# Row maxima transposed in float32 and split when they leave PSUM, and gelu rows evicted by ScalarE, in a gated attention and mixing kernel

## The chip, the cores and the metric

The kernel runs on one core of a Trainium2 chip. The metric is the device time of one launch in microseconds, as the median of several runs. A core has TensorE (PE, its weight loads shown as PEld), VectorE (DVE), ScalarE (ACT), GpSimd (POOL), and SyncE (SP), which here only issues DMAs. Each engine works through its own queue in order and waits on semaphores for the others.

## The reference, cut to what matters

`x` is 8 x 512 x 2048, `ctx` has the same shape. Two layers follow each other, each with a layernorm over the 2048 columns in front and a gated addition behind:

```python
x = x + tanh(g_xattn[0]) * xattn(layernorm(x), ctx, mask, Wq, bq, Wk, bk, Wv, bv, Wo, bo)
x = x + tanh(g_ffn[0]) * ffn(layernorm(x), W_res, W_pre, W_post, ..., W_branch)
```

The attention cuts the 2048 columns into patches of 128. In a patch, q and k come from the normalised x and v from ctx; 8 heads of 32 channels attend within the patch:

```python
scores = einsum('bhdi,bhdj->bhij', qh, kh) / sqrt(dh)
scores = where(mask > 0, scores, -1e9)
attn = softmax(scores, axis=-1)
o = gelu(einsum('bhij,bhdj->bhdi', attn, vh).reshape(BN, DK, W), approximate=False)
out = einsum('de,bew->bdw', Wo, o) + bo[:, None]
```

The second layer takes each row of 2048 as 4 streams of 512. It computes 24 logits of a row (16 for a 4x4 matrix, 4 + 4 for two softmaxes), makes the matrix doubly stochastic by 50 Sinkhorn iterations, and mixes the streams with it. A weighted sum of the streams goes through `W_branch` and is added to each stream with its own weight.

## The kernel before, in words

The work is cut into 32 blocks of 512 columns (`n`), 4 per batch element, and each block into 4 patches of 128 columns, 128 patches in all (`t`). One loop runs over `t` and, for each, goes through the string `ORDER = "MeoaMgPlsMMvSMpOM"`, whose letters call the stages: `s` the score maxima of patch `t + 3` (`smax`), `e` the exponentials of patch `t` (`expo`), `a` the sums over values of patch `t - 1` (`attv`), `g`, `o` and `O` the output projection of the block before (`outp`), `p` and `P` the q and k projection of a later block (`proj`) and its restacking through DRAM (`stack`), `v` the value projection (`vproj`), `S` the row sums and logits of a later batch element (`stats`), `M` steps of the mixing of an earlier batch element (`mix`). At the last block of a batch element its logits are finished (`rawmap`) and its Sinkhorn chain (`ffn`) is put in at a priority of its own. A scheduler then orders each engine's instructions by priority and by its own model of times, so the order of every queue is made anew whenever an instruction changes.

**Score maxima.** `smax` multiplies the stacked q and k of a patch (16-bit, 97 rows) head by head into one PSUM tile `sc` of 128 x 8 x 128 (L569, 8 matmuls) and VectorE takes the maximum over each row (L571, `mx`, 128 rows x 8 heads). VectorE scales it and rounds it to float16 (L573), and takes the rest that this loses as a second float16 part (L574); both lie in `mq`, 128 x 16. TensorE transposes `mq` into the first 16 partitions of the same `sc` tile, seen as float16 (L576), and ScalarE copies that to `mh`, 16 x 128 (L578). Two DMAs on SyncE's queue put the two halves of `mh` into rows 97 and 98 of the stacked q (L582). `expo` then multiplies 99 rows (L595, tile `sT`), so that the row maximum is subtracted within the matmul, and ScalarE takes the exponential (L597, `e`). `sc` and `sT` come from one pool of two PSUM buffers (`ps_s`).

**Projection.** For each quarter of the q and k rows TensorE makes 12 matmuls (L518 to L520) into `qk`, ScalarE writes the first float16 part of the result (L522) and VectorE the second (L523, both into `ev`). The activations are split the same way before: GpSimd normalises (L500, `xn`), ScalarE casts (L505, `xh`), GpSimd subtracts (L507, `xl`).

**Attention.** TensorE sums the exponentials and their products with the values (L612, L616, tile `u`), ScalarE makes the reciprocal by a logarithm and an exponential (L618, L619, `rc`), and VectorE multiplies (L620, `o`).

**Output.** ScalarE applies gelu to a block of `o` (L627) between two loads of its function table, GpSimd multiplies by the mask (L632). TensorE transposes the 8 squares of 128 x 128 in two groups (L641, `gTp`, in the pool `ps_t` of two PSUM buffers), and VectorE copies each group of 128 x 512 to `gT` (L642). Four matmuls with the logit weights follow (L645). ScalarE rounds `o` (L655, `gh`), GpSimd takes the rest (L657, `gl`), TensorE makes the output projection (L667 to L670), VectorE adds it to x (L671), ScalarE sums the squares (L673).

**Second layer.** A Sinkhorn sweep is six small VectorE instructions (L844, L846, L848, L850, L852, L854) that depend on each other; 49 sweeps for each of 8 batch elements. The mixing uses VectorE (L946, L949), ScalarE (L939) and GpSimd (L944); for some tiles of the late batch elements it runs on TensorE instead (L1000, L1001).

Of the kernel before, what the change touches and what calls it, by code (L numbers as in the profile page):

```python
# [11 lines left out]
F16 = mybir.dt.float16  # L12
BF16 = mybir.dt.bfloat16
AF = mybir.ActivationFunctionType
ALU = mybir.AluOpType
# [4 lines left out]
P = 128  # L20
D = 512
S = 2048
DK = 256
NH = 8
# [12 lines left out]
MH_ACT = False  # L37
# [54 lines left out]
M_UNIT = 16384.0  # L92
# [7 lines left out]
def gated_xattn_mhc_kernel(  # L100
# [21 lines left out]
    V, A, G, T, SY = nc.vector, nc.scalar, nc.gpsimd, nc.tensor, nc.sync  # L122
# [6 lines left out]
    def ctile(shape, dt, name):  # L129
        return const.tile(shape, dt, tag=name, name=name)  # L130


    ident = ctile([P, P], F32, "ident")
# [8 lines left out]
    ident16 = ctile([P, P], F16, "ident16")  # L142
# [49 lines left out]
    mp = ctx.enter_context(tc.tile_pool(name="mp", bufs=BUF_MP))  # L192
# [10 lines left out]
    def defer(k, tag, fn):  # L203
        if k == 0:
            fn()
        else:
            late.append([k, fn, tag])
# [49 lines left out]
    with tc.tile_pool(name="set", bufs=1) as st:  # L257

        def stile(shape, dt, name, tag=None):
            return st.tile(shape, dt, tag=tag or name, name=name)  # L260
# [64 lines left out]
        for t in range(2):  # L325
            sl = slice(256 * t, 256 * t + 256)
# [21 lines left out]
        mh = stile([B * 16, 3, P], BF16, "mh")  # L348
# [213 lines left out]
    def smax(t):  # L562

        m, p = divmod(t, PSB)
        q, kk = QS[m % NS], KS[m % NS]
        sl = slice(p * P, (p + 1) * P)
        sc = ps_s.tile([P, NH, P], F32, tag="s", name="smax")
        for h in range(NH):
            T.matmul(sc[:, h, :], q[0:97, h, sl], kk[0:97, h, sl], start=True, stop=True)  # L569
        mx = mp.tile([P, NH], F32, tag="mx", name="mx")  # L570
        V.tensor_reduce(mx, sc, AX.X, ALU.max)  # L571
        mq = mp.tile([P, 2, NH], F16, tag="mq", name="mq")
        V.tensor_scalar(mq[:, 0, :], mx, 1.0 / M_UNIT, None, ALU.mult)  # L573
        V.scalar_tensor_tensor(mq[:, 1, :], mx, 1.0 / M_UNIT, mq[:, 0, :], ALU.mult, ALU.subtract)  # L574
        mt = sc[0 : 2 * NH, 0, :].bitcast(F16)[:, 0:P]
        T.transpose(mt, mq.rearrange("p r h -> p (r h)"), ident16)  # L576
        mh = mp.tile([2 * NH, P], F16, tag="mh", name="mh")
        A.copy(mh, mt)  # L578

        def put():  # L580
            for r in range(2):
                (A if MH_ACT else SY).dma_start(q[97 + r : 98 + r, :, sl], mh[r * NH : (r + 1) * NH, :])  # L582

        defer(D_MH, t, put)

# [36 lines left out]
    def outp(n):  # L622

        b, k = divmod(n, NBLK)
        o = ob.pop(n)
        for g in range(2):
            gi = A.activation(o[:, g], o[:, g], AF.Gelu, bias=bvc[:, g : g + 1])  # L627
        with tc.issue_after(gi.ins), tc.high_priority():
            A.preload_act_table_set(EXP_SET)
        mb = gp.tile([P, BLK], F32, tag="mb", name="mb")  # L630
        SY.dma_start(mb, mask[b, k * BLK : (k + 1) * BLK].partition_broadcast(P))
        G.tensor_tensor(o, o, mb.unsqueeze(1).broadcast_to([P, 2, BLK]), ALU.mult)  # L632
        j0 = n * NP
        gt_ = op_.tile([P, NP, DK + 1], F32, tag="gT", name="gT")
        G.tensor_copy(gt_[:, :, DK], maskT[:, j0 : j0 + NP])
        yield
        for q in range(2):
            pt = ps_t.tile([P, 2, 2, P], F32, tag="t", name="gTp")
            for j in range(2):
                for e in range(2):  # L640
                    T.transpose(pt[:, j, e, :], o[:, e, (2 * q + j) * P : (2 * q + j + 1) * P], ident)  # L641
            V.tensor_copy(gt_[:, 2 * q : 2 * q + 2, 0:DK], pt.rearrange("p j e s -> p j (e s)"))  # L642
        g4 = ps_t.tile([P, DK + 1], F32, tag="t", name="g4")
        for p in range(NP):
            T.matmul(g4[32 * p : 32 * p + 32, :], Wm[:, k * NP + p, :], gt_[:, p, :], start=True, stop=True)  # L645
        if k == 0:
            g4s = lnp.tile([P, DK + 1], F32, tag="g4s", name="g4s", bufs=2)
            V.tensor_copy(g4s, g4)
            G4[b] = g4s
        else:  # L650
            V.tensor_tensor(G4[b], g4, G4[b], ALU.add)
        mr = MR[n % 2]
        SY.dma_start(mr[0:6, :], mrow_d[:, n * BLK : (n + 1) * BLK])
        gh = gp.tile([P, 2, BLK], F32R, tag="gh", name="gh")
        A.copy(gh, o)  # L655
        gl = gp.tile([P, 2, BLK], F32R, tag="gl", name="gl")
        G.tensor_tensor(gl, o, gh.bitcast(F32), ALU.subtract)  # L657
        if k == 0:
            sq2[b] = lnp.tile([P, 4, NBLK], F32, tag="sq2", name="sq2")
            x1s[b] = x1d.tile([D, S], F32, tag="x1s", name="x1s")  # L660
        xt = xtile.pop(n)
        yield
        for c in range(4):
            ps = ps_p.tile([P, BLK], F32, tag="p", name="op")
            cs = slice(c * P, (c + 1) * P)
            for e in range(2):
                T.matmul(ps, WoH[:, e, cs], gh[:, e], start=(e == 0), stop=False)  # L667
                T.matmul(ps, WoH[:, e, cs], gl[:, e], start=False, stop=False)  # L668
                T.matmul(ps, WoL[:, e, cs], gh[:, e], start=False, stop=False)  # L669
            T.matmul(ps, bo6[:, cs], mr, start=False, stop=True)  # L670
            V.tensor_tensor(xt[c], ps, xt[c], ALU.add)  # L671
            jk = fp.tile([P, BLK], BF16, tag="ph", name="junk2", bufs=BUF_PH)
            A.activation(jk, xt[c], AF.Square, bias=nmean[b][:, c : c + 1], accum_out=sq2[b][:, c, k : k + 1])  # L673
            defer(D_X1, "x1", lambda cs=cs, c=c: SY.dma_start(x1s[b][cs, k * BLK : (k + 1) * BLK], xt[c]))
            yield
# [341 lines left out]
    for t in range(2):  # L1017
        smax(t)
# [4 lines left out]
    for t in range(2, AHEAD):  # L1023
        smax(t)
# [22 lines left out]
    def act(c, t):  # L1047
# [8 lines left out]
        elif c == "a" and 1 <= t <= NT_:  # L1056
            at("attv", attv, t - 1)
        elif c == "g" and p == 0 and n >= 1:
            og_[0] = outp(n - 1)
            at("outp", next, og_[0])  # L1060
        elif c == "P" and live_ and n + 1 < NTOT:
# [6 lines left out]
        elif c == "l" and live_:  # L1068
# [4 lines left out]
            if p == LXP and n > 1 and n + 2 < NTOT:  # L1073
                defer(D_LX, "lx", lambda n=n: load_x(n + 2))
        elif c == "s" and live_ and t + AHEAD < NT_:
            at("smax", smax, t + AHEAD)
        elif c == "v" and live_:
            if t + 2 < NT_ and t % 2 == 0:
# [117 lines left out]
```

## Time and profile before

| what | us |
|---|---|
| median of 3 runs | 1831.41 |
| lowest and highest of them | 1829.26, 1835.13 |
| the profiled execution | 1828.05 |
| its span, first to last instruction | 1825.9 |
| mean granted TensorE clock | 0.932 of full speed |
| score maxima (L571), first and last start | 73.0, 1595.7 |

The profile is of one execution on the core. A row of instructions names the line, the engine, the operation, the tile written and the tiles read, the shapes, how many there are, their busy time and mean duration, and then how long the engine sat idle before them and who ended that. A row of waits names the one that waits, the one that ended the wait, the total in us, how many times, and the longest. A slice row gives the busy share of an engine in 40 equal slices of the span, in tenths, where 9 is 90% or more; one slice is 45.6 us. The ends of TensorE's matmuls are modelled, so their rows can overlap. The score maxima end near 1600 us; what follows is the last Sinkhorn chain and the mixing of the last batch elements.

### The profile page before, as it was taken

What the parts mean: (1) busy time and instruction counts of PE and PEld (TensorE: products, weight loads), DVE (VectorE), ACT (ScalarE), POOL (GpSimd) and SP (SyncE); (2) the same over time, 40 slices, a digit from 0 to 9 for tenths busy, and PEclk for the clock granted to TensorE, in tenths of its full rate; (3) what the DMA queues carried; (4) which work ended last, traced back from release to release, by engine and by line L of the source; (5) the groups of instructions that cost most, each with busy time, mean ns of one, the idle gap of its engine ahead of it and who ended that gap; (6) DMA issues with size and microseconds to landing.
All of it is one profiled execution on the core that took longest, in us unless ns stands there. A gap on an engine that the chain in (4) does not pass through costs nothing.

```text
span 1825.9 us, 32268 instructions
## 1 busy us (share of the span) xinstructions
PE 1547.1 (85%) x10517; PEld 901.0 (49%) x10517; DVE 1382.3 (76%) x4201; ACT 1069.4 (59%) x2030; POOL 602.8 (33%) x511
## 2 busy tenths in 40 slices
PE   3998999989889888889878888799888889768887
PEld 2554555555555554545544445455455555543333
DVE  7434345877888778888888879889898998998761
ACT  2386466646555656558565475566665566755454
POOL 0512222322232243342444333444334442321121
PEclk7999999999999988999988999899999999989999
DMA  6478696467646855568555784468755565523443
GB/s 214 139 209 256 208 258 194 140 174 232 180 134 200 254 169 165 151 192 269 162 154 164 214 251 144 139 196 259 215 154 165 148 189 147 172 93 119 144 157 117
DMA packets 353237, 330.60 MB, mean 181 GB/s; under 512 B 53351, under 2 KB 251303, under 8 KB 353070
## 3 DMA queue, kind: packets, MB, share of 16 engines
q1 hardware_dynamic: 353070, 328.55, 60.6%
q8 instruction: 83, 1.36, 0.3%
q14 instruction: 84, 0.69, 0.1%
HBM read 226.71 MB, written 101.16 MB: 180 GB/s over the span
## 4 chain that ended last, share of the span: by engine, by line
PE 37%; DVE 23%; DMA 18%; issue 9%; ACT 9%; POOL 4%; SPq 1%; ACTq 0%; POOLq 0%; DVEq 0%
PE vp L559 5%; DVE w L946 4%; DMA xs<-in_x_dram 4%; PE qk L518 3%; PE qk L519 3%; DMA out_dram<-w 3%; PE qk L520 3%; DMA x<-x1s 2%; PE mx L1000 2%; DMA x1s<-xt 2%; PE lgx L448 2%; DVE mx L571 2%; PE op L667 2%; DVE W L844 2%; PE mx L1001 2%
## 5 line engine op out<-in xcount | busy, mean ns | idle before, releaser
L559 PE MATMUL vp<-Wv,ct 128*128 128x256 f32 x1024 | 272.4, 418 | 16.7 <-DMA ct<-in_cx_dram 15.1
L500 POOL TENSOR_SCALAR xn<-xt,ln_r,nb 128x512 f32<-128x512 f32 x128 | 105.5, 826 | 501.2 <-DMA xt<-in_x_dram 385.7
L559 PEld LDWEIGHTS vp<-Wv,ct 128*128 128x128 f32 x1024 | 207.4, 210 | 68.0 <-issue 18.6
L518 PE MATMUL qk<-xh,WqkH 128*128 128x512 f16 x512 | 199.2, 390 | 29.4 <-ACT xh L505 16.3
L946 DVE SCALAR_TENSOR_TENSOR w<-x,Et,w 128x512 f32<-128x512 f32 x180 | 180.0, 1001 | 49.6 <-POOL w L944 34.0
L519 PE MATMUL qk<-xl,WqkH 128*128 128x512 f16 x512 | 197.9, 387 | 4.3 <-POOL xl L507 4.0
L520 PE MATMUL qk<-xh,WqkL 128*128 128x512 f16 x512 | 197.6, 386 | 0.0
L571 DVE TENSOR_REDUCE mx<-smax 128x8 f32<-128x1024 f32 x128 | 154.9, 1210 | 41.7 <-PE smax L569 41.3
L507 POOL TENSOR_TENSOR xl<-xn,xh 128x512 f16<-128x512 f32 x128 | 156.3, 1228 | 76.0 <-ACT xh L505 70.4
L597 ACT ACTIVATE e<-sT,ebi,esc 128x1024 f32<-128x1024 f32 x128 | 153.4, 1198 | 18.0 <-PE sT L595 17.9
L523 DVE SCALAR_TENSOR_TENSOR ev<-qk,bqs,ev 128x512 f16<-128x512 f32 x128 | 94.5, 739 | 77.5 <-ACT ev L522 76.1
L667 PE MATMUL op<-gh,WoH 128*128 128x512 f32 x256 | 120.9, 474 | 35.3 <-DVE ev L523 31.1
L944 POOL TENSOR_TENSOR w<-w,pj 128x512 f32<-128x512 f32 x60 | 80.1, 1334 | 213.1 <-ACT w L939 113.7
L505 ACT CAST xh<-xn 128x512 f16<-128x512 f32 x128 | 78.3, 612 | 103.7 <-POOL xn L500 102.9
L522 ACT ACTIVATE ev<-qk,bqs 128x512 f16<-128x512 f32 x128 | 86.9, 679 | 85.0 <-PE qk L520 78.7
L673 ACT ACTIVATE junk<-xt,nmean 128x512 bf16<-128x512 f32 x128 | 91.6, 716 | 73.9 <-DVE xt L671 41.3
L850 DVE TENSOR_TENSOR W<-E,uv 128x64 f32<-128x64 f32 x392 | 119.4, 307 | 5.4
L844 DVE TENSOR_TENSOR W<-E,uv 128x64 f32<-128x64 f32 x352 | 117.1, 335 | 4.8
L612 PE MATMUL u<-e,onesb 128*32 128x256 f32 x1024 | 102.7, 403 | 10.5 <-DVE mq L573 3.8
L668 PE MATMUL op<-gl,WoH 128*128 128x512 f32 x256 | 107.1, 418 | 0.0
L669 PE MATMUL op<-gh,WoL 128*128 128x512 f32 x256 | 106.6, 417 | 0.0
L632 POOL TENSOR_TENSOR o<-o,mb 128x1024 f32<-128x1024 f32 x32 | 75.6, 2364 | 93.2 <-ACT o L627 85.9
(287 smaller groups left out, 3504.6 us busy)
## 6 DMA issues: line engine op xcount, KB each, us to landing
xt<-in_x_dram SPq DMA_DIRECT2D x128, 256.0 KB
ct<-in_cx_dram SPq DMA_DIRECT2D x128, 256.0 KB
xTt<-in_xT_dram SPq DMA_DIRECT2D x128, 256.0 KB
qd<-ev SPq DMA_DIRECT2D x128, 256.0 KB
x1s<-xt SPq DMA_DIRECT2D x128, 256.0 KB
xs<-in_x_dram SPq DMA_DIRECT2D x112, 256.0 KB
QS<-qd SPq DMA_DIRECT2D x192, 128.0 KB
KS<-qd SPq DMA_DIRECT2D x192, 128.0 KB
```

The source lines that it names most:

```text
L507: G.tensor_tensor(l, xn, h, ALU.subtract)
L518: T.matmul(ps, WqkH[:, c, ms], hs[c], start=(c == 0), stop=False)
L519: T.matmul(ps, WqkH[:, c, ms], ls[c], start=False, stop=False)
L520: T.matmul(ps, WqkL[:, c, ms], hs[c], start=False, stop=(c == 3))
L559: T.matmul(ps[:, h, :], ct[:, c, :], Wv[:, c, :], start=(c == 0), stop=(c == 3))
L571: V.tensor_reduce(mx, sc, AX.X, ALU.max)
L597: A.activation(e32, sc, AF.Exp, bias=ebi[:, t : t + 1], scale=esc[:, t : t + 1])
L667: T.matmul(ps, WoH[:, e, cs], gh[:, e], start=(e == 0), stop=False)
L668: T.matmul(ps, WoH[:, e, cs], gl[:, e], start=False, stop=False)
L844: V.tensor_tensor(W4[:, h], E4[:, h], vb[:, h], ALU.mult)
L850: V.tensor_tensor(W4[:, h], E4[:, h], ub[:, h], ALU.mult)
L946: V.scalar_tensor_tensor(w, x1[j], E[:, n, 4 * j + i : 4 * j + i + 1], w, ALU.mult, ALU.add)
```

## The change

Two places change.

In `smax`, the maxima go to TensorE as they are, in float32, and come out of PSUM in two float16 parts. ScalarE scales and rounds while it copies; VectorE then computes the rest from the same PSUM rows and ScalarE's part. The tile `mq` and its two VectorE instructions are gone. `mh` is now 8 partitions x 2 x 128, and each DMA takes one part of it.

In `outp`, the transposed gelu rows are copied out of PSUM by ScalarE and not by VectorE.

```diff
         mx = mp.tile([P, NH], F32, tag="mx", name="mx")
         V.tensor_reduce(mx, sc, AX.X, ALU.max)
-        mq = mp.tile([P, 2, NH], F16, tag="mq", name="mq")
-        V.tensor_scalar(mq[:, 0, :], mx, 1.0 / M_UNIT, None, ALU.mult)
-        V.scalar_tensor_tensor(mq[:, 1, :], mx, 1.0 / M_UNIT, mq[:, 0, :], ALU.mult, ALU.subtract)
-        mt = sc[0 : 2 * NH, 0, :].bitcast(F16)[:, 0:P]
-        T.transpose(mt, mq.rearrange("p r h -> p (r h)"), ident16)
-        mh = mp.tile([2 * NH, P], F16, tag="mh", name="mh")
-        A.copy(mh, mt)
+
+        mt = sc[0:NH, 0, :]
+        T.transpose(mt, mx, ident)
+        mh = mp.tile([NH, 2, P], F16, tag="mh", name="mh")
+        A.activation(mh[:, 0, :], mt, AF.Copy, scale=1.0 / M_UNIT)
+        V.scalar_tensor_tensor(mh[:, 1, :], mt, 1.0 / M_UNIT, mh[:, 0, :], ALU.mult, ALU.subtract)
 
         def put():
             for r in range(2):
-                (A if MH_ACT else SY).dma_start(q[97 + r : 98 + r, :, sl], mh[r * NH : (r + 1) * NH, :])
+                (A if MH_ACT else SY).dma_start(q[97 + r : 98 + r, :, sl], mh[:, r, :])
...
-            V.tensor_copy(gt_[:, 2 * q : 2 * q + 2, 0:DK], pt.rearrange("p j e s -> p j (e s)"))
+            A.copy(gt_[:, 2 * q : 2 * q + 2, 0:DK], pt.rearrange("p j e s -> p j (e s)"))
```

In the changed kernel the transpose is L574, ScalarE's part L576, VectorE's L577 and the DMAs L581; lines further down stand one lower than before, so the gelu copy is L641.

## The prediction

> **What bounds the kernel now.** I read the page's busy shares first, then the slices, then one steady stretch by itself, and last who ends TensorE's idle time in it. The busy shares and two of the slice rows:
>
> ```profile
> PE 1547.1 (85%) x10517; PEld 901.0 (49%) x10517; DVE 1382.3 (76%) x4201; ACT 1069.4 (59%) x2030; POOL 602.8 (33%) x511
> PE   3998999989889888889878888799888889768887
> DVE  7434345877888778888888879889898998998761
> ```
>
> TensorE looks like the bound, but its ends are modelled. Start to start, two 16-bit matmuls of 512 columns lie 0.216 us apart where their rows show 0.39 us, so its 85% is overstated. VectorE's rows hardly overlap, and from the eighth slice on it is at 7 tenths or more, mostly 8 or 9, until the last two. The stretch from 330 to 1530 us, where attention tiles, projections, the Sinkhorn sweeps and the mixing of a finished batch all interleave, by itself:
>
> ```profile
> 330.00:1530.00 1200.00, 1026.69 (x7353) 624.63 (x7352) 1010.28 (x2939) 730.48 (x1407) 452.65 (x371) 0.93 0.63 186
> ```
>
> The columns are length, busy PE, PEld, DVE, ACT, POOL, granted clock, DMA share, GB/s. VectorE works 1010 of 1200 us; 190 us are left. TensorE's waits in the stretch that bear on this change (total us, times, longest):
>
> ```profile
> PE op L667 <- DVE ev L523: 29.5, 20, 4.9
> PE g L645 <- DVE gT L642: 17.2, 10, 3.9
> PE smax L576 <- DVE mq L574: 6.3, 4, 3.3
> ```
>
> Adding all of TensorE's waits of the stretch by the engine that ended them, VectorE ended 85.0 of 171.7 us, ScalarE 40.1, DMA 29.8, GpSimd 16.8. So VectorE is the engine that TensorE most often finds late, and about half of what VectorE loses or gains there should reach the end. I use one half for VectorE and ScalarE time. For TensorE's own time I take 0.45: its matmul rows are 37% of the chain that ended last, 676 us, against 1547 us busy.
>
> VectorE's rows of the stretch (busy us, mean ns, idle before it and who ended that):
>
> ```profile
> L571 DVE TENSOR_REDUCE mx<-smax 128x8 f32<-128x1024 f32 x95 | 114.8, 1208 | 15.5 <-PE smax L569 15.1
> L523 DVE SCALAR_TENSOR_TENSOR ev<-qk,bqs,ev 128x512 f16<-128x512 f32 x95 | 70.0, 737 | 30.2 <-ACT ev L522 29.0 <-DMA xt<-in_x_dram 0.5
> L620 DVE TENSOR_TENSOR o<-u,rc 128x256 f32<-128x256 f32 x93 | 38.1, 410 | 17.5 <-ACT rc L619 15.1 <-issue 2.1
> L642 DVE COPY gT<-gTp 128x512 f32<-128x512 f32 x48 | 31.8, 674 | 3.0 <-PE gTp L641 2.9
> L573 DVE TENSOR_SCALAR mq<-mx 128x8 f16<-128x8 f32 x95 | 29.6, 312 | 0.1
> L574 DVE SCALAR_TENSOR_TENSOR mq<-mx,mq 128x8 f16<-128x8 f32 x94 | 27.0, 287 | 0.0
> ```
>
> **VectorE, removed and changed.** In the built order its instructions fall from 4203 to 4011, which is 128 (L573) and 64 (L642); ScalarE's rise from 1792 to 1856. In the stretch L573 takes 29.6 us with it and L642 31.8 us. L574 stays as an operation, but now reads 8x128 out of PSUM. No row has that shape; the low end is its own 154 ns median. The high end: 256 columns take 410 (L620) and 512 take 674 (L671), so 128 would take about 280, and the one 128x128 two-input row (L271) shows 275. I take 280, by the nearest width: 94 x 0.28 = 26.3 us, as much as the 27.0 now.
>
> But the means of the two small rows are not work. Minimum, median and maximum in the stretch (ns):
>
> ```profile
> L573 DVE TENSOR_SCALAR mq<-mx x95: 96/161/2301, 340.6 to 1529.2; 128x8 f16<-128x8 f32 x95
> L574 DVE SCALAR_TENSOR_TENSOR mq<-mx,mq x94: 97/154/2306, 341.7 to 1517.8; 128x8 f16<-128x8 f32 x94
> L844 DVE TENSOR_TENSOR W<-E,uv x247: 154/224/2369, 330.8 to 1519.8; 128x64 f32<-128x64 f32 x124
> ```
>
> Some last 2.3 us, as long as GpSimd's 128x1024 operations (2364 to 2411 ns). The excess over the median is 14.3 us for L573 and 12.5 us for L574. The Trainium skill, "SBUF — State Buffer", section "Who interferes with whom", says that a VectorE instruction with two SBUF inputs, or in a two-port mode, shares a port with GpSimd and is held up, and one with at most one SBUF input outside those modes is not. By the rule both stalls go, since the new split reads PSUM and one SBUF tile: -29.6 - 31.8 - 0.7 = -62 us. By the L844 row they largely move: the sweeps behind it have two SBUF inputs, stall in the same way (mean 360, median 224), and would meet the same GpSimd operation. If all moves, it is -(95 x 0.161) - 31.8 + 94 x (0.280 - 0.154) = -15.3 - 31.8 + 11.8 = -35 us. I take -42, nearer the second.
>
> **The new wait on VectorE.** The second split needs ScalarE's first (`mh[:, 0]`), so the path is now VectorE, TensorE, ScalarE, VectorE, and VectorE works in order: behind a late split stand Sinkhorn steps most often (about 80 of 128 times in the built order), else the next maximum, the normalised output L620 or `ev`. The trace has waits of this kind: L523 on ScalarE's half costs 29.0/95 = 0.31 us, L620 15.1/93 = 0.16 us. Below zero is excluded, as VectorE has no such wait there now. I take 0.31, the same construction: 95 x 0.31 = +29 us. Net VectorE: -42 + 29 = -13 us, half of it **-6.5 us**.
>
> **TensorE.** The transpose now moves 128 float32 columns. Start to start, float32 transposes (L641) lie 0.109 us apart, 16-bit matmuls of 128 columns 0.055 us; 128 x 0.054 = 6.9 us, times 0.45 is **+3 us**. Below nothing is excluded, unless 8 weight columns load faster than 16 (85 ns today), which is less than this. Two small VectorE steps ahead of it become none: 10 us of waits on mq (6.3 on L574, 3.8 on L573 by L612) shrink, **-3 us**.
>
> **ScalarE.** L578 (243 ns, 16x128) becomes an 8x128 copy with a scale, same width: nothing. The gT copies add 48 x 0.589 = 28 us in the stretch (L560 and L985, 128x512 out of PSUM, 589 and 586 ns). A rule speaks against it: the skill's "ScalarE: Activation LUTs", "Rules for kernel authors", gives simple arithmetic to VectorE, which it calls up to about 3 times faster in its packed 16-bit modes. The rows decide otherwise here: the source is float32 in PSUM, VectorE needs 674 ns, ScalarE 589. By the rule the move would lose time on both counts; by the rows it saves 85 ns each and unloads the busier engine. ScalarE is busy 730 of 1200, so most of it is covered by 464 us of idle time. Without that cover, 3.8% more load on the 116 us for which TensorE and VectorE wait for ScalarE is 4 us, half of it **+2 us**. Behind a gT copy on ScalarE stand mostly the `gh` cast or an `xh` cast. TensorE's 17.2 us wait for gT becomes a wait on the less busy engine: between 0 and -17 in TensorE time, I take half of it at one half, **-4 us**.
>
> **SyncE.** Each tile still issues two DMAs of 0.64 us. The second now waits for VectorE, and in 42 of 128 tiles other issues stand between the two (5 before). Behind it stand loads of ct and of the stacked Q and K; TensorE waits 13.2 us for ct and 7.9 us for KS. From the second issue to the tile's first sT matmul there are 9.4 us in nine tiles of ten (2.0 at the least), so I take 0 and keep +5. The score buffer in PSUM is held to the split's end, not mh's: 8.9 us (median) of a 12.6 us tile now; 0, up to +5.
>
> **Sum:** -6.5 + 3 - 3 + 2 - 4 = -8.5 us. The profiled execution took 1828.05 us (span 1825.9 and 2.2 around it), so 1819.5 for its like; the median is 3.4 us higher, hence 1831.4 - 8.5 = **1823 us**.
>
> **Rivals.**
> - *VectorE sets the whole pace of the stretch.* The stalls vanish (-62), the new wait is as small as L620's (+15), and two thirds pass on: -31, with TensorE's +3 about 1803 us. For it speaks that VectorE is 84% busy; against it that TensorE waits for three other engines as well.
> - *The loop of four hops makes VectorE wait (slower).* Today the time from the end of L574 to the end of mh is 4.7 us on average (2.8 until TensorE takes the transpose, 1.7 until ScalarE does, 0.24). In the built order only 12 instructions, about 3.6 us of VectorE work behind the maximum, precede the split (median). If the hops stay as long, VectorE stands 1.1 us each time: 95 x 1.1 = 105, less 42, half of it +31, 1861 us. At 0.85 us it is 1849 us. It decides from 42/95 = 0.44 us of wait each. Against it: TensorE takes the transpose much earlier in the new order (29 matmuls behind the scores, not 51).
> - *Nothing moves out:* what VectorE gains comes back as idle time behind ScalarE and DMA: 1828 to 1836 us.
> - That it does not do what it says is excluded by the built order. But every queue's order is built anew, and differs from the first tiles on; what that alone does, no row tells. It widens each case by some 8 us.
>
> **Numbers.** Relief as summed (1823) 0.32, full pace (1803) 0.18, nothing 0.16, the wait (about 1849) 0.34. A measurement of this kernel tells about 0.3%, 5.5 us, from no change. Faster 0.50, same 0.16, slower 0.34. The likeliest case alone spans 1812 to 1830; the range, reaching to the other cases, 1797 to 1855.
>
> **What would show it.** Right: VectorE busy down by some 50 us in all, L571's count unchanged, the split at 0.28 us without 2.3 us outliers, its wait on ScalarE under 0.44 us each; gT on ScalarE at 0.59 us; TensorE's waits on `ev` and gT down. Wrong: a row of VectorE waiting for mh of 60 us or more, more TensorE idle time behind KS, QS or ct, or sweeps (L844, L850 of before) that grow by as much as the small rows lost.

## The result, and the profile after

The changed kernel takes 1858.77 us (median of 4 runs, 1849.04 to 1860.67); the kernel before took 1832.09 us beside it (4 runs, 1829.26 to 1835.13). The ratio is 1.0142, with a 95% interval of 1.0107 to 1.0176: slower by 26 us, where the forecast was 8 us faster. The profiled execution took 1859.74 us, its span is 1858.0 us, and the mean granted TensorE clock is 0.921 (0.932 before).

The busy shares and the two slice rows of the page, after:

```profile
PE 1552.2 (84%) x10454; PEld 912.8 (49%) x10517; DVE 1370.0 (74%) x4009; ACT 1103.4 (59%) x2094; POOL 602.1 (32%) x511
PE   3989889988899787888878888788787888868887
DVE  7334235777778788778888878888898878988762
```

192 instructions left VectorE (4201 to 4009), but its busy time fell by 12.3 us only. ScalarE's 64 new copies are all there. The stretch from 330 to 1530 us, columns as before:

```profile
330.00:1530.00 1200.00, 1012.96 (x7236) 623.21 (x7284) 981.75 (x2777) 740.95 (x1429) 441.48 (x363) 0.92 0.62 182
```

In the same 1200 us every engine but ScalarE is busy for less time, and TensorE makes fewer weight loads, 7284 where it was 7352. (The matmul counts can't be compared: this trace lacks 63 of the run's 10517 matmul records.) TensorE's waits in the stretch (total us, times, longest):

```profile
PE op L666 <- DVE ev L523: 37.8, 20, 4.0
...
PE smax L574 <- DVE mx L571: 12.7, 15, 4.0
...
PE smax L569 <- DVE mh L577: 7.9, 5, 2.5
...
PE g L644 <- ACT gT L641: 4.9, 5, 2.1
```

The wait for gT fell from 17.2 to 4.9 us as hoped. The wait for `ev` rose from 29.5, the 6.3 us on `mq` became 12.7 us on the reduction itself, and a wait for the new split is there. The new split and the first sweep row in that stretch, minimum, median and maximum in ns:

```profile
L577 DVE SCALAR_TENSOR_TENSOR mh<-smax,mh x93: 216/272/279, 337.8 to 1516.2; 8x128 f16<-8x128 f32 x93
```

```profile
L843 DVE TENSOR_TENSOR W<-E,uv x250: 153/224/2396, 331.4 to 1521.7; 128x64 f32<-128x64 f32 x125
```

And three VectorE rows of the whole run (busy us, mean ns, idle before it):

```profile
L849 DVE TENSOR_TENSOR W<-E,uv 128x64 f32<-128x64 f32 x392 | 137.0, 350 | 6.6
L843 DVE TENSOR_TENSOR W<-E,uv 128x64 f32<-128x64 f32 x352 | 125.0, 356 | 5.8
...
L577 DVE SCALAR_TENSOR_TENSOR mh<-smax,mh 8x128 f16<-8x128 f32 x128 | 34.4, 269 | 40.4 <-ACT mh L576 38.9 <-DMA KS<-mneg_d 0.8
```

The split never lasts longer than 279 ns: reading PSUM, it isn't held up. The two sweep rows together grew from 236.5 to 262.0 us, as if the stalls had moved there; e9 and e11 below show that the order of the queues alone makes them grow almost as much. VectorE stands 38.9 us in the whole run for ScalarE's part, 0.30 us each; 16.3 us of it lie in the stretch.

**Where the 32 us of span went.** Cut at the reductions of patches 0, 96 and 127, the kernel before needs 1143.6 us for the first 96 patches and 379.1 us for the other 31; after, 1148.8 and 400.3. (From the last reduction to the end it is 230.2 and 236.5.) So two thirds of the loss lie in the last 31 patches. Those 31 in the kernel before, after, and (a run told below) in the kernel before with the same instructions in another order; each line is of its own trace, columns as above:

```profile
1216.60:1595.70 379.10, 329.55 (x2433) 205.19 (x2432) 336.94 (x1009) 240.47 (x459) 151.68 (x122) 0.93 0.62 181
```

```profile
1221.10:1621.40 400.30, 331.47 (x2378) 205.86 (x2393) 347.94 (x965) 244.36 (x467) 153.26 (x123) 0.91 0.58 170
```

```profile
1197.20:1608.40 411.20, 337.00 (x2362) 208.07 (x2377) 348.78 (x1010) 238.06 (x457) 150.73 (x124) 0.91 0.58 166
```

The second number is TensorE's busy time: within 8 us in all three. Adding up TensorE's gaps of 0.15 us and more in these stretches gives 48.6, 67.8 and 72.9 us. Of the 20 profiles of this study (18 experiments, before and after), the kernel before has the shortest such stretch; the others need 384.2 to 418.0 us. (In the reordered kernel the mixing starts a patch sooner: its first 96 patches take 1125.3 us, 18 less, and it gives back more.) That is the first sign that the kernel before holds an unusually well fitting order there, and not only that the change broke something. The new wait of VectorE for ScalarE's part does not lie where the time went: 35.6 us of it are in the first 96 patches, which lost 5 us, and 3.4 us in the last 31, which lost 21.

### The profile page after: what moved, and what is told of

Read it like the earlier page. It is cut to its first block, busy times and chain, and to the rows that moved or that the text cites. A ratio compares the mean times of both kernels' runs of the same rounds, so it can differ in the third digit from the quotient of the medians.

```text
span 1858.0 us, 32254 instructions
## 1 busy us (share of the span) xinstructions
PE 1552.2 (84%) x10454; PEld 912.8 (49%) x10517; DVE 1370.0 (74%) x4009; ACT 1103.4 (59%) x2094; POOL 602.1 (32%) x511
## 4 chain that ended last, share of the span: by engine, by line
PE 37%; DMA 19%; DVE 18%; ACT 9%; issue 9%; POOL 4%; SPq 2%; another core or an unknown queue 0%; POOLq 0%; ACTq 0%; DVEq 0%
PE vp L559 6%; DVE w L945 3%; DMA xt<-in_x_dram 3%; DMA ct<-in_cx_dram 3%; PE qk L518 3%; PE qk L519 3%; PE qk L520 2%; DMA xs<-in_x_dram 2%; DMA x1s<-xt 2%; PE lgx L448 2%; PE mx L999 2%; DMA out_dram<-w 2%; PE mx L1000 2%; DVE W L843 2%; PE op L666 2%
## 5 line engine op out<-in xcount | busy, mean ns | idle before, releaser
L518 PE MATMUL qk<-xh,WqkH 128*128 128x512 f16 x512 | 201.9, 395 | 29.7 <-ACT xh L505 20.1
L571 DVE TENSOR_REDUCE mx<-smax 128x8 f32<-128x1024 f32 x128 | 155.2, 1212 | 45.1 <-PE smax L569 44.8
L596 ACT ACTIVATE e<-sT,ebi,esc 128x1024 f32<-128x1024 f32 x128 | 153.4, 1199 | 12.8 <-PE sT L594 12.8
L849 DVE TENSOR_TENSOR W<-E,uv 128x64 f32<-128x64 f32 x392 | 137.0, 350 | 6.6
L843 DVE TENSOR_TENSOR W<-E,uv 128x64 f32<-128x64 f32 x352 | 125.0, 356 | 5.8
L569 PE MATMUL smax<-KS,QS 97*128 97x128 f16 x1024 | 87.0, 224 | 33.8 <-DMA KS<-qd 16.1
L670 DVE TENSOR_TENSOR xt<-op,xt 128x512 f32<-128x512 f32 x128 | 86.3, 675 | 35.3 <-PE op L669 19.2
```

Source lines behind the costliest of these rows:

```text
L518: T.matmul(ps, WqkH[:, c, ms], hs[c], start=(c == 0), stop=False)
L596: A.activation(e32, sc, AF.Exp, bias=ebi[:, t : t + 1], scale=esc[:, t : t + 1])
L843: V.tensor_tensor(W4[:, h], E4[:, h], vb[:, h], ALU.mult)
L849: V.tensor_tensor(W4[:, h], E4[:, h], ub[:, h], ALU.mult)
```

## The experiments

All ratios are against the kernel before, measured beside each run on the same chip, with 95% intervals. "Before" and "after" in the table name the kernel that was edited. Every run is an edit and also a new order of all queues; how much the order alone can do is seen only from e9 on, so what e1 to e8 and e13 to e16 say of a cause is a hint and not a proof.

| run | what it is | us | ratio |
|---|---|---|---|
| e1 | maxima change alone | 1854.50 | 1.0092 (1.0070 to 1.0114) |
| e2 | gelu copies alone | 1843.28 | 1.0031 (1.0018 to 1.0045) |
| e3 | VectorE makes both parts from PSUM | 1865.97 | 1.0153 (1.0127 to 1.0180) |
| e4 | ScalarE leaves PSUM in float32, VectorE's part from SBUF | 1843.83 | 1.0029 (1.0012 to 1.0045) |
| e5 | e1 with two idle steps ahead of the transpose | 1870.92 | 1.0157 (1.0139 to 1.0175) |
| e6 | before, transpose in float32 | 1851.55 | 1.0058 (1.0041 to 1.0075) |
| e7 | before, second part left out | 1851.71 | 1.0060 (1.0038 to 1.0083) |
| e8 | whole change with e5's steps | 1869.82 | 1.0157 (1.0136 to 1.0177) |
| e9 | before, EARLY 5 | 1846.70 | 1.0040 (1.0021 to 1.0059) |
| e10 | after, EARLY 5 | 1867.82 | 1.0146 (1.0110 to 1.0182) |
| e11 | before, LAGS 29 | 1848.16 | 1.0046 (1.0030 to 1.0062) |
| e12 | after, LAGS 29 | 1858.17 | 1.0096 (1.0066 to 1.0126) |
| e13 | whole change with e4's split | 1845.69 | 1.0042 (1.0025 to 1.0060) |
| e14 | e1, VectorE makes both parts from SBUF | 1904.39 | 1.0374 (1.0344 to 1.0405) |
| e15 | before, and an idle VectorE copy out of PSUM | 1841.94 | 1.0017 (1.0000 to 1.0034) |
| e16 | before, and an idle VectorE copy out of SBUF | 1860.59 | 1.0140 (1.0111 to 1.0170) |
| e17 | e13, EARLY 5 | 1889.57 | 1.0276 (1.0237 to 1.0316) |
| e18 | e13, LAGS 29 | 1851.26 | 1.0077 (1.0050 to 1.0105) |

None beats the kernel before.

### Which part costs (e1, e2)

e1 is the change without the edit of the gelu copies, e2 is that edit alone:

```diff
-            V.tensor_copy(gt_[:, 2 * q : 2 * q + 2, 0:DK], pt.rearrange("p j e s -> p j (e s)"))
+            A.copy(gt_[:, 2 * q : 2 * q + 2, 0:DK], pt.rearrange("p j e s -> p j (e s)"))
```

> Only the maxima change; the gelu rows still leave PSUM by VectorE. Theory A (the loop TensorE, ScalarE, VectorE of the maxima costs: later release of the score buffer, VectorE waiting for ScalarE): most of the +26.7 us is here, 1852 to 1862 us. Theory B (the gelu copies in ScalarE's queue hold up what stands behind them): 1828 to 1836 us here. Theory C (neither alone; what the two do to the order together): both halves within 8 us of 1832.

> Only the gelu rows leave PSUM by ScalarE; the maxima are as before. Theory A: 1820 to 1832 us, a small gain from 43 us less on VectorE. Theory B: 1850 to 1862 us. Theory C: within 8 us of 1832.

Measured: +0.92% and +0.31%. Both are slower by themselves, though e2 only takes 64 copies from the busier engine. About two thirds of the loss come with the maxima.

### The way over ScalarE (e3, e4)

e3 has no step of ScalarE between the two of VectorE; e4 takes PSUM out of VectorE's hands. Both with the gelu copies on VectorE:

```diff
 # e3
-        A.activation(mh[:, 0, :], mt, AF.Copy, scale=1.0 / M_UNIT)
+        V.tensor_scalar(mh[:, 0, :], mt, 1.0 / M_UNIT, None, ALU.mult)
 # e4
-        A.activation(mh[:, 0, :], mt, AF.Copy, scale=1.0 / M_UNIT)
-        V.scalar_tensor_tensor(mh[:, 1, :], mt, 1.0 / M_UNIT, mh[:, 0, :], ALU.mult, ALU.subtract)
+        m32 = mp.tile([NH, P], F32, tag="m32", name="m32")
+        A.activation(m32, mt, AF.Copy, scale=1.0 / M_UNIT)
+        A.copy(mh[:, 0, :], m32)
+        V.tensor_tensor(mh[:, 1, :], m32, mh[:, 0, :], ALU.subtract)
```

> Maxima transposed in float32 as in the change, but VectorE makes both float16 parts out of PSUM, so that ScalarE is not in the chain; gelu rows by VectorE. VectorE gets 128 x about 0.25 us more than in the change. Theory A (the hop over ScalarE is what costs): clearly below the run with the maxima change alone, 1830 to 1842 us in spite of 30 us more VectorE work. If the float32 transpose or the later release after VectorE is what costs: as slow as that run, or slower. Theory B: no difference expected from the hop, 1835 to 1845 us by the added VectorE work alone.

> Maxima transposed in float32; ScalarE takes them out of PSUM once, scaled and in float32, then rounds the first part from SBUF; VectorE takes the rest from SBUF. PSUM is free after ScalarE's first instruction, and VectorE still waits for ScalarE. Theory A in the form that the late release of the score buffer costs: 1830 to 1840 us. Theory A in the form that VectorE's wait costs: as slow as the maxima change alone, about 1855 us, or slower by ScalarE's 30 us more.

Measured: +1.53% and +0.29%. Taking the hop away does not help, which speaks against the hop as the cost. In e4 VectorE waits 42.5 us for ScalarE, more than in the change, and e4 is among the fastest, which speaks against the wait. Each is one order only.

### The place of the transpose in TensorE's queue (e5 to e8)

The order of TensorE's queue showed another difference. Before, a median of 35 matmuls stands between a patch's scores and its transpose in the order as built; after, 22 (counted in the traces, 44 and 28). If a late reduction stops TensorE there, more matmuls between should help. e5 and e8 put two VectorE copies between reduction and transpose (e5 with the gelu copies on VectorE); e6 keeps every step of before and makes only the columns and the transpose float32; e7 leaves the second part out.

```diff
 # e5, e8
+        mx0 = mp.tile([P, NH], F32, tag="mxc0", name="mq0")
+        V.tensor_copy(mx0, mx)
+        mx1 = mp.tile([P, NH], F32, tag="mxc1", name="mq1")
+        V.tensor_copy(mx1, mx0)
-        T.transpose(mt, mx, ident)
+        T.transpose(mt, mx1, ident)
 # e6 (against before)
-        mq = mp.tile([P, 2, NH], F16, tag="mq", name="mq")
+        mq = mp.tile([P, 2, NH], F32, tag="mq", name="mq")
-        T.transpose(mt, mq.rearrange("p r h -> p (r h)"), ident16)
+        T.transpose(mt, mq.rearrange("p r h -> p (r h)"), ident)
 # e7 (against before)
-        V.scalar_tensor_tensor(mq[:, 1, :], mx, 1.0 / M_UNIT, mq[:, 0, :], ALU.mult, ALU.subtract)
```

> The change of the maxima alone, with two VectorE copies of the 8 maxima (128x8) put between the reduction and the float32 transpose: they carry nothing new, but the transpose stands in TensorE's queue about as late behind the score matmuls as before the change (a median of 34 matmuls between, 35 before, 22 with the maxima alone). Theory D (what costs is that the transpose follows the reduction too closely in TensorE's queue, so that TensorE stalls on a late reduction): the idle time of TensorE in front of the transposes' loads that the reduction ends (21 us after the change) goes below 3 us, and the ratio to before is 1.000 to 1.004, though VectorE is given 30 to 60 us more work than with the maxima alone. Theory F (the float32 transpose, the release of its PSUM buffer by VectorE's step and the clock cost, wherever it stands): 1.009 or more, as with the maxima alone, or above it for the added VectorE work.

> The kernel before with its two VectorE steps and its one ScalarE copy kept, but their 16 columns held and transposed in float32 (the first part isn't rounded, so that the second is zero: the result lacks the second part's purpose). The order in TensorE's queue stays (35 matmuls between). Theory D: a float32 transpose costs what its row says, some 0.05 us more on TensorE 128 times, at most 7 us in all: ratio 1.000 to 1.004. Theory F: the float32 transpose itself costs 10 to 17 us: ratio 1.006 to 1.010.

> The kernel before without its second VectorE step: only the first float16 part is made and transposed (8 columns), the second row of each head is filled from a tile of zeros, so that the result leaves out the second part. VectorE loses 128 instructions of about 0.27 us (some 34 us) and gains nothing; the transpose stands earlier in TensorE's queue (a median of 30 matmuls between, 17 in a tenth). Theory D: the gain of VectorE's work is eaten by the earlier transpose: ratio 0.997 to 1.004, with TensorE waiting on the first part's step by more than before. Theory F: nothing costs here, so VectorE's 34 us count in part: ratio 0.985 to 0.995.

> The whole change, with the two VectorE copies of the maxima put between the reduction and the transpose as in the run with the maxima alone (33 matmuls between). Theory D: what is left is the cost of the gelu copies alone, ratio 1.001 to 1.006. Theory F: 1.012 or more, as the change. If the two parts only add whatever the order, the ratio is that of the cushion run plus 0.003.

Measured: 1.0157, 1.0058, 1.0060, 1.0157. In e5 and e8 the transposes stand as late as before (a median of 45 and 43 matmuls behind the scores in the traces) and the kernel is slower than without the two steps, so the place in the queue by itself is not seen to cost. But the stall that theory D blames was not taken away: the weight loads of the transposes still waited 24.3 us in e5 and 20.8 in e8, now for the second copy, where they had waited 21.4 us for the reduction in the changed kernel and 11.0 for `mq` before; under 3 us had been expected. So D in the form of that stall was not tested. The rival (F), that the float32 transpose itself costs, has e6's 0.58%, no more than 0.2% above what order alone does below. That e8 equals e5 suggests that the parts don't add: the gelu copies' 0.31% is not there. e7 is the odd one: it has 127 VectorE instructions fewer than the kernel before and, but for one tile of zeros, nothing added; yet VectorE's busy time is 7.5 us longer (1389.8) and the kernel is slower. No account of added work explains that.

### The order by itself (e9 to e12)

So the work was left alone and only the order moved, by one constant of the schedule at a time, in the kernel before and in the changed one:

```diff
 # e9, e10
-EARLY = 4
+EARLY = 5
 # e11, e12
-LAGS = (30,) * 8
+LAGS = (29,) * 8
```

> The kernel before, with the row sums of a later batch element started one patch sooner (EARLY 5, was 4): not one instruction more or less, but 64% of TensorE's matmuls and 88% of VectorE's instructions stand at another place of their queue (by 7 and 11 places in the mean, from early on). Theory O (the order of before is a lucky or a tuned one, and any new order of the queues costs): ratio 1.003 to 1.012 with the same work. Theory W (the changed instructions themselves cost): 0.998 to 1.002.

> The changed kernel with the same setting (EARLY 5): the changed instructions, again another order (60% of the matmuls stand elsewhere). Theory O: the time is drawn anew, so it may lie well off the change's, from 1.000 to 1.016, and its distance to before's kernel with the same setting is no longer 1.014 but within 0.006 of 1. Theory W: 1.012 to 1.016, as the change.

> The kernel before, with the mixing of a finished batch element started one patch sooner (LAGS 29, was 30): the same instructions, 54% of the matmuls and 69% of VectorE's instructions at another place, by 10 places in the mean, from a third of the way on. Theory O: ratio 1.002 to 1.010. Theory W: 0.998 to 1.002.

> The changed kernel with LAGS 29. Theory O: between 1.002 and 1.016, its distance to before's kernel with the same setting other than 1.014 by more than 0.004. Theory W: 1.012 to 1.016, and 1.012 to 1.016 over before's kernel with the same setting.

Measured: the kernel before loses 0.40% and 0.46% with not one instruction changed. The changed kernel is at 1.0142, 1.0146 and 1.0096 in its three orders. The distance between the two at the same setting is 1.0142, 1.0106 (1.0146/1.0040) and 1.0050 (1.0096/1.0046); the last two are uncertain by about 0.004 and 0.003, an estimate from the two intervals of each. So order alone is worth 7 to 8 us against the kernel before; something of the 26 us is left in each pair, between 9 and 26 us. Neither theory was right in full: the order (O) explains what happened to the kernel before, the changed instructions (W) the changed kernel at EARLY 5.

The order also changes how busy VectorE is. The busy shares of e9, e10, e11 and e12, and the sweep rows of the two without the change (e9, then e11):

```profile
PE 1532.6 (83%) x10455; PEld 899.9 (49%) x10517; DVE 1411.8 (77%) x4201; ACT 1067.7 (58%) x2030; POOL 603.9 (33%) x511
PE 1537.9 (83%) x10454; PEld 912.0 (49%) x10517; DVE 1373.3 (74%) x4009; ACT 1104.3 (60%) x2094; POOL 601.2 (32%) x511
PE 1542.3 (84%) x10451; PEld 903.9 (49%) x10517; DVE 1402.8 (76%) x4201; ACT 1068.4 (58%) x2030; POOL 593.5 (32%) x511
PE 1549.1 (83%) x10452; PEld 911.8 (49%) x10517; DVE 1368.5 (74%) x4009; ACT 1105.6 (59%) x2096; POOL 600.8 (32%) x511
```

```profile
L850 DVE TENSOR_TENSOR W<-E,uv 128x64 f32<-128x64 f32 x392 | 134.0, 342 | 6.1
L844 DVE TENSOR_TENSOR W<-E,uv 128x64 f32<-128x64 f32 x352 | 121.4, 345 | 6.0
```

```profile
L844 DVE TENSOR_TENSOR W<-E,uv 128x64 f32<-128x64 f32 x352 | 131.5, 376 | 5.3
L850 DVE TENSOR_TENSOR W<-E,uv 128x64 f32<-128x64 f32 x392 | 128.3, 331 | 5.7
```

With the same 4201 instructions VectorE is busy for 1411.8 and 1402.8 us, where it was 1382.3 in the kernel before: its sweeps stall more (255.4 and 259.8 us, 236.5 before), while the two small steps keep their 73 and 71 us. At the same setting the change takes 12.3, 38.5 and 34.3 us off VectorE's busy time, and the sweeps grow by 25.5, 12.8 and 11.1 us. So at most that much of their growth can be put down to the change, and the small gain of the measured pair comes in good part from the kernel before, whose order has fewer of VectorE's stalls than the other two.

### Release of PSUM, or the wait (e13 to e16)

Two candidates for what is left: VectorE, late in its queue, now releases the score buffer in PSUM; or VectorE stands waiting for ScalarE. e13 is the whole change with e4's split; e14 is e1 with both VectorE steps reading `m32` in SBUF. e15 and e16 add one unused copy to the kernel before, of PSUM and of SBUF:

```diff
 # e14
-        A.activation(mh[:, 0, :], mt, AF.Copy, scale=1.0 / M_UNIT)
-        V.scalar_tensor_tensor(mh[:, 1, :], mt, 1.0 / M_UNIT, mh[:, 0, :], ALU.mult, ALU.subtract)
+        A.activation(m32, mt, AF.Copy, scale=1.0 / M_UNIT)
+        V.tensor_copy(mh[:, 0, :], m32)
+        V.tensor_tensor(mh[:, 1, :], m32, mh[:, 0, :], ALU.subtract)
 # e15 (against before)
         A.copy(mh, mt)
+        V.tensor_copy(jv, mt[0:NH])
 # e16 (against before)
         A.copy(mh, mt)
+        V.tensor_copy(jv, mh[0:NH])
```

> The whole change, but ScalarE takes the scaled float32 rows out of PSUM into SBUF (m32) and rounds the first part from there, and VectorE makes the rest from two SBUF tiles: PSUM is released by ScalarE, VectorE still waits for ScalarE. Theory R (beyond a new order, 0.4%, what costs is that the score buffer in PSUM is let go by VectorE, late in its queue): 1.002 to 1.007. Theory V (VectorE's standing wait in the loop of hops costs, wherever it reads): 1.010 to 1.016, as the change.

> The maxima change alone, ScalarE copies the scaled float32 rows to SBUF, and VectorE makes both parts from there, so it has as many steps behind the transpose as in the run in which it made both from PSUM (ratio 1.0153), but PSUM is released by ScalarE. Theory R: 1.003 to 1.008. Theory V: 1.012 to 1.017, since wait and work on VectorE are the same or more.

> The kernel before with one VectorE copy of 8x128 float16 added, which reads the transposed maxima in PSUM beside ScalarE's copy and whose result nobody uses: the score buffer is let go by VectorE too. Some 0.2 us of VectorE work 128 times (25 us), no wait on ScalarE. Theory R: 1.010 to 1.016, and by 0.004 or more above its twin that reads SBUF. Theory V: 1.004 to 1.010, not above its twin.

> The twin of the run before it: the same added VectorE copy of 8x128 float16, but of mh in SBUF, so that VectorE waits for ScalarE and PSUM is released by ScalarE as before. Theory R: 1.003 to 1.008 (a new order and 25 us of VectorE work, part of it). Theory V: 1.008 to 1.016, at least as high as its twin, for the longer wait.

Measured: 1.0042, 1.0374, 1.0017, 1.0140. The added copy of e15, and then of e16, with what it waited for (us, times):

```profile
L580 DVE COPY jv<-smax x128: 148/204/214, 79.1 to 1609.1; 8x128 f16<-8x128 f16 x128
its engine sat idle before it (us, times) until:
  ACT mh L578: 44.8, 27
```

```profile
L580 DVE COPY jv<-mh x128: 118/176/2350, 78.3 to 1637.5; 8x128 f16<-8x128 f16 x128
its engine sat idle before it (us, times) until:
  ACT mh L578: 48.2, 26
```

e15 turned out to have both: VectorE releases the buffer and also waits 44.8 us for ScalarE. That kernel has 20.5 us more of VectorE's busy time (1402.8, as much as e11 has with nothing added) and 44.8 us of wait, 65 us in all, and it is 3 us slower. VectorE's gaps of 0.15 us and more between 60 and 1640 us add up to 322.5 us, where it was 325.8 before: the new wait took the place of others. So in this kernel neither the release (R) nor the wait (V) costs, and VectorE's time has no fixed price. For the changed kernel V is not excluded in the same way: its gaps come to 363.0 us, 37 more than before. R does not explain e14, in which ScalarE releases the buffer and which is the slowest of all; why it is, is not settled. e16 differs in one thing that the rows show, the stalls up to 2.35 us of a copy whose both ends are in SBUF, but it also has its own order (71% of the matmuls stand elsewhere than in e15), so its 1.40% can't be put down to them. e13, at 1.0042, made it look as if the split from SBUF were the cheap one.

### The same work in three orders (e17, e18)

> The whole change with the split from SBUF (ScalarE takes float32 out of PSUM and rounds, VectorE makes the rest), in a second order of the queues (EARLY 5, was 4). Theory P (the split as the change makes it costs some 0.7% whatever the order, the split from SBUF does not): 1.002 to 1.008, below the change at the same setting (1.0146) by 0.006 or more. Theory O (only the order matters, and 1.0042 was a good draw): anywhere from 1.003 to 1.016, as likely above 1.009 as below.

> The same in a third order (LAGS 29, was 30). Theory P: 1.001 to 1.008, below the change at the same setting (1.0096) by 0.003 or more. Theory O: anywhere from 1.003 to 1.016, as likely above the change at that setting as below it.

Measured: 1.0276 and 1.0077, so e13's instructions cost 0.4%, 2.8% or 0.8% by their order. The advantage of the split from SBUF falls: over three orders it averages 1.0132, the change 1.0128, the kernel before 1.0029. The pages of e13 and e17:

```profile
span 1847.6 us, 32372 instructions
...
PE 1553.5 (84%) x10517; PEld 915.8 (50%) x10517; DVE 1374.0 (74%) x4009; ACT 1132.0 (61%) x2224; POOL 603.8 (33%) x511
```

```profile
span 1892.6 us, 32359 instructions
...
PE 1552.4 (82%) x10452; PEld 918.7 (49%) x10517; DVE 1379.6 (73%) x4009; ACT 1126.7 (60%) x2222; POOL 604.1 (32%) x511
```

The busy times agree within 6 us on every engine, and the spans differ by 45 us. What differs is TensorE's idle time between 60 and 1680 us (231.9 and 267.3) and the time at half the clock (297.7 and 351.3 us, from the clock's records in the traces). Idle time behind DMA and ScalarE grew most (63.3 to 85.0 and 45.2 to 71.0); no single wait carries it. The time at half the clock does not set the kernel's time by itself: e18 has 244.9 us of it and a span of 1848.2 us, e13 297.7 us and 1847.6.

EARLY and LAGS each move a whole stage by one patch, so they are not a blind shuffle of the queue. e17's loss can be the price of earlier row sums beside this split; e10, the change at the same setting, does not show it.

## Why the prediction was wrong

**The step that failed first: the order was taken as +-8 us on both sides.** The prediction said "what that alone does, no row tells. It widens each case by some 8 us". The runs tell it: for the kernel before, a new order cost +7 and +8 us in two of two tries. That fits a kernel whose order is unusually good, with the shortest last 31 patches of all 20 profiles and the least VectorE busy time of its three orders; two tries do not prove it. For one set of instructions a changed order was worth up to 2.3% (e13 to e17), 43 us. A sum of -8.5 us from rows had no hold against that.

**VectorE's relief, -42 us in the stretch, was mis-sized for this pair of orders.** The single rows were right: the split takes 272 ns (280 taken) and has no 2.3 us outliers. The rule of the Trainium skill's "SBUF — State Buffer", section "Who interferes with whom", holds for the instruction itself (214 ns at most when e15's copy reads PSUM, 2350 ns when e16's reads SBUF) but says nothing on where the stall goes. In the stretch the sweeps grew from 177.5 us for 521 of them to 201.9 us for 529, some 22 us; the small rows had 26.8 us in excess. That looks like stalls that moved, but e9 and e11 have it in large part with the small steps still there. What was wrong besides is "VectorE's rows hardly overlap". This is one stall of the kernel before on VectorE, and GpSimd's row at the same time (start, duration):

```profile
1163.23 0.24 DVE L854 RECIPROCAL uv<-sm 128x16 f32<-128x16 f32 x1
1163.39 0.17 DVE L852 TENSOR_REDUCE sm<-W 128x16 f32<-128x64 f32 x1
1163.48 1.49 DVE L946 SCALAR_TENSOR_TENSOR w<-x,Et,w 128x512 f32<-128x512 f32 x1
1164.90 2.30 DVE L573 TENSOR_SCALAR mq<-mx 128x8 f16<-128x8 f32 x1
1167.11 0.21 DVE L844 TENSOR_TENSOR W<-E,uv 128x64 f32<-128x64 f32 x1
```

```profile
1164.39 2.78 POOL L657 TENSOR_TENSOR gl<-o,gh 128x1024 fp32r<-128x1024 f32 x1
```

L573 ends at 1167.20, with GpSimd's row at 1167.17. And each VectorE row starts some 0.08 us before the one ahead has ended. Over the run the durations add up to 1608.0 us, the busy time to 1382.3. The two small steps add up to 72.7 us by duration, but cover only 41.6 us alone; the gelu copies 43.3 and 35.1; the new split 34.4 and 20.0. The two sweep rows came back with 31.4 us that nothing else covers, all six rows of a sweep together with 46.1. -41.6 - 35.1 + 20.0 + 46.1 = -10.6 us; the page shows -12.3, and the rest is spread over other rows.

**The new wait, +29 us in the stretch, was too high there:** it took 16.3 us, 0.18 us each. The 0.31 us each that were taken fit only the whole run (38.9 us, 0.30 each). For like work, take the 94 patches between the 28th maximum and the 122nd, which fill the stretch before. The change in VectorE's busy time, plus the new wait, is -13.6 + 16.5 = +3 us in them, where -13 was forecast. At EARLY 5 it is -24.0 + 11.4 = -13 us and at LAGS 29 -33.1 + 21.4 = -12 us. So the sum forecast for VectorE came out in two orders, by luck, since two errors offset each other there (a relief of 24 and 33 us where 42 was taken, a wait of 11 and 21 where 29 was); it missed in the measured order.

**The share of one half fell altogether.** In the two orders in which VectorE's account fell by 12 to 13 us, the change is still 1.06% and 0.50% slower. What VectorE gained came back as idle time: from the first maximum to the last it stands idle for 339.6 us before and 382.5 after, 331.8 and 381.6 at EARLY 5, 338.2 and 389.4 at LAGS 29. Nor does the account follow the time elsewhere: e15 has 65 us more of it and loses 3 us; e7 has 7.5 us more and loses 11; e13, e17 and e18 have the same account (busy time and wait for mh) within 11 us and lie 43 us apart.

**TensorE.** The float32 transpose at +3 us is not contradicted: e6 has +0.58%, of which a new order alone is 0.4%. "mq waits shrink, -3" was wrong: without the two steps the transpose moved up to the reduction, and 6.3 us (and 3.8 on L573's) became 12.7. **ScalarE** was right: gT at 578 ns, TensorE's wait for it 12 us shorter; yet e2 shows no gain, +0.31%, a little less than what a new order costs. **SyncE:** TensorE's waits on KS and ct in the stretch went from 7.9 to 11.0 and from 13.2 to 17.3 us, 7 us together, a little over the +5 kept.

**The rivals.** The loop of four hops was the slower one, with 1849 us, deciding at 0.44 us of wait each. The wait stayed at 0.30 (0.18 in the stretch), under that point, so by its own working this rival did not decide; e3, which has no such wait, is slower too. That its number lies nearest to the measured one is luck. The full pace fell. The rival that nothing moves out had the idle time right, and not the loss.

**What stays open.** A changed order alone is shown to cost the kernel before 0.4% to 0.5%. The 0.5% to 1.4% between the two kernels at the same setting are measured, but whether the changed instructions cost that, and by which wait, or three unlucky orders do, can't be told with a spread of 2.3% for one set of instructions. A run of the changed instructions pinned to the old order was not tried, nor were more than three orders of any kernel.

## What to carry to other kernels

When a scheduler makes every queue anew, run the old kernel in two or three other orders first: that shows how much of a difference is only order, and whether the kernel to be beaten holds a lucky one. Compare busy times and stalls of old and new at the same setting in several orders, since they change with the order too. Price a removed VectorE instruction by the time that it covers alone and not by its row. A change whose sum is smaller than the spread of orders is not forecast by its rows.

## What the runs showed of the hardware that was not expected

- VectorE's rows overlap by a median of 0.082 us, 2858 times in the kernel before; 4201 rows of 1608.0 us make 1382.3 us busy.
- VectorE's busy time changes with the order of the queues: 1382.3, 1411.8 and 1402.8 us for the same 4201 instructions (before, e9, e11).
- TensorE's time at half the clock changes with the order too: 249.3 us before and 295.3 after, and 244.9 to 351.3 us over three orders of the same instructions (e18, e17), in one profiled execution each. The matmuls that start in it go from 808 to 1147 between those two. Executions of one kernel differ as well: the mean granted clock was 0.925 to 0.940 in e18, 0.918 to 0.930 in e13 and 0.908 to 0.914 in e17, so only e17 stands apart.
